# Attention with a condition token: turning blocks of x later, one head's row scores ahead in all phases, the maxima split between two halves of an exchange

## The chip, the cores and the metric

The kernel runs on one core of one Trainium2 chip. The metric is the device time of one execution in microseconds (us); lower is better. Three runs of the kernel before took 650.82 to 651.73 us, the median is 651.13 us. The profile comes from one execution of its own, which took 652.28 us; its span, from the first to the last instruction, is 650.4 us. In the profile PE is TensorE's matmuls, PEld its weight loads, DVE VectorE, ACT ScalarE, POOL GpSimd, SP SyncE.

## What is computed

x is (8, 512, 512) in float32: 8 batches, 512 positions, 512 channels in 16 heads of 32. A condition token per batch adds its own projections to queries and keys, and the attention's output is added to x.

```python
Q = _split_heads(x @ Wq.T + bq)
K = _split_heads(x @ Wk.T + bk)
V = _split_heads(x @ Wv.T + bv)
tQ = _split_heads(tokens @ Wq.T + bq)
tK = _split_heads(tokens @ Wk.T + bk)
cQ = Q + tQ
cK = K + tK
scores = jnp.einsum('bhqd,bhkd->bhqk', cQ, cK) / jnp.sqrt(jnp.float32(HEAD_DIM))
attn = jax.nn.softmax(scores, axis=-1)
out = jnp.einsum('bhqk,bhkd->bhqd', attn, V)
return out.transpose(0, 2, 1, 3).reshape(B, S, D_MODEL)
...
x = x + _L0_cond_ref(x, cond_1024[:, None, :], L0_cond_Wq, L0_cond_bq, L0_cond_Wk, L0_cond_bk, L0_cond_Wv, L0_cond_bv)
```

## The kernel before

**Groups and phases.** Four heads make a group; 8 batches of 4 groups give 32 groups t = 0 to 31. The groups run as a pipeline written out by hand: every engine executes its instructions in the order in which the program emits them, and waits on semaphores for what it needs. A start covers the first projections and group 0, then the function thirds (from L1152) runs once for each of t = 1 to 28, and a tail written out for the last three groups ends the kernel. One call of thirds is called a phase here. Even and odd are by t; r is t modulo 4.

**Row scores, maxima, denominators.** For the softmax each row's maximum is needed first. row_scores (L640) computes the scores of 128 queries by 512 keys of one head into one bank of PSUM; four heads take four banks. VectorE takes the negated maxima (one_max, L592, one bank; row_max_of, L649, two neighbouring banks at once). denominators (L700) has ScalarE compute exp(score + negated maximum) with the sum along the row. For the first two of four query blocks these exponentials are kept in SBUF (the tile store) and used; for the other two only the sums are.

**Kept exponentials and the exchange.** The kept ones lie with queries on the partitions, and the product with V needs keys there. turn_kept (L659) turns blocks of 32 by 32 on VectorE; then swap_kept (L681) exchanges the blocks between partition groups by DMA in three rounds (move 0: part to a place aside; move 1: counterpart to part; move 2: aside to counterpart), each of six DMAs of 128 KB. Move 1 is issued by SyncE, move 2 by GpSimd, move 0 by both: with `later = 6 if t % 4 == 1 else 2`, the first 2 (or all 6) by SyncE and the rest by GpSimd. Each DMA waits for the round before it to land.

**The other half.** For the last two query blocks the scores are computed again, transposed: the maxima have been split into three bfloat16 parts by four small GpSimd instructions (split_max, L714 to L717), turned by one DMA that SyncE issues (turn_max, L726), and less_max (L771) adds them into PSUM by a matmul; scores_of_rest (L784) adds the scores, and ScalarE takes the exponential (rest_leaves, L798). In odd phases joined does this for i = 1 and puts row scores of one head (number 1) between less_max and the first scores_of_rest, and the other three heads' row scores before the last of them. In even phases exponentials_of_rest comes first and all four heads' row scores behind it.

**One phase** has three parts. i = 0: row scores and maxima of group t + 1's query blocks 1 and 2, then the product with V of group t - 1 (weighted: L839 sums, L874 spreads the denominators, L911 turns the result, L912 and L913 scale it and add x, L916 stores it), then one of the items of projection. i = 1 and i = 2: the second half's exponentials of group t, the row scores of (t + 1, block 3) and (t + 2, block 0), and one more item each. The projections (L461) of the next batch are spread over four phases in twelve items (MADE), each six to eight small products of a Strassen-like scheme; q, k and v items end in VectorE, ScalarE or GpSimd instructions (first_by_others, L529 to L540; other_products, L554 and L486; other_shared, L1230 to L1236). The last L486 of an even phase's i = 1 makes the keys that the row scores of i = 2 read.

**Banks.** The eight banks of PSUM go round by lists: row_of says which bank has which role in a part, released(...) says in which order the roles pass on to the next, and begin(...) moves a pair of neighbouring banks to the end of each four.

**x.** Blocks of x come by four DMAs each (load_block, L173, SyncE), two tiles in turn; turn_x (L371) turns one block into xT on VectorE. turn_more calls it once per phase, in i = 0, behind weighted (place (0, 2)); load_blocks right behind it loads the block after next into the tile that has just been read, which waits for the turn. combine_x has GpSimd make sums of parts of xT in every fourth phase. The tile pool xtp has two tiles for xT, taken in turn by batches. So SyncE's queue has in each phase: its share of moves 0 and 1, four stores of the result, four loads of x, the DMA that turns the maxima, four loads of the residual (L191), in this order.

Of the kernel before, what the change touches and what calls it, by code (L numbers as in the profile page):

```python
# [9 lines left out]
F32 = mybir.dt.float32  # L10
# [7 lines left out]
def kernel(  # L18
# [38 lines left out]
    nc = tc.nc  # L57
# [18 lines left out]
    xp = ctx.enter_context(tc.tile_pool(name="xp", bufs=2))  # L76
    xtp = ctx.enter_context(tc.tile_pool(name="xtp", bufs=2))
    qkp = ctx.enter_context(tc.tile_pool(name="qkp", bufs=3))
# [268 lines left out]

    xT = {}

    def transpose_x(n, pt, leaves=nc.vector.tensor_copy):  # L350

        b, sc = divmod(n, NS)
        if b >= B:
            return
        if sc == 0:
            xT[b] = xtp.tile([P, NC, S], F32, tag="xT", name=f"xT_{b}")
        for cc in range(NC):
            nc.tensor.transpose(
                pt[:, cc * P : (cc + 1) * P], xs[n][:, cc * P : (cc + 1) * P], ident
            )  # L360
        leaves(xT[b][:, :, sc * P : (sc + 1) * P], pt.rearrange("p (c s) -> p c s", c=NC))
        if n > 1:
            load_block(n + 2)

    def turn_x(n):
        b, cc = divmod(n, NC)
        if b >= B:
            return
        if cc == 0:
            xT[b] = xtp.tile([P, NC, S], F32, tag="xT", name=f"xT_{b}")  # L370
        nc.vector.transpose(xT[b][:, cc, :], xs[n].rearrange("p f i -> p (f i)"))  # L371
        to_load.append(n + 2)

    to_load = []

    def load_blocks():
        while to_load:
            load_block(to_load.pop(0))
# [701 lines left out]
    bias_residual(1)  # L1080
    turn_x(NC + 3)
    load_blocks()
    advance()
# [3 lines left out]
    other_products("v", 0, 0, nothing, nothing, (0, 2))  # L1087
    turn_kept(1, 0)
    advance()
# [4 lines left out]
    first_products("v", 0, 1, lambda: denominators(1, 3), nothing, 1)  # L1094
    turn_kept(1, 1)
    turn_kept(1, 2)
# [43 lines left out]
    TURNED_LAST = {(0, 2): 2, (1, 2): 2}  # L1140
    turned = {}

    def turn_more(t, i, after):

        for _ in range((TURNED if t + 1 < KEPT[-1] else TURNED_LAST).get((i, after), 0)):
            if t + 1 in KEPT:
                n = turned[t + 1] = turned.get(t + 1, -1) + 1
                turn_kept(t + 1, n)
        if (i, after) == (0, 2):
            turn_x((t - 1) % G + ((t - 1) // G + 2) * NC)  # L1150

    def thirds(t, made):  # L1152
# [12 lines left out]
        turn_more(t, 0, 2)  # L1165
        load_blocks()
        one_item(of, *next(made), (2, 3), ignore, nothing)
        released(0, 1, 4, 5, 6, 7, 2, 3)
        for i in (1, 2):
            begin(HG)  # L1170
            rows = (t + 1, 3) if i == 1 else (t + 2, 0)
            if i == 1 and r % 2 == 1:
                joined(t, i - 1, rows)
# [7 lines left out]
            if i == 1:  # L1181
                first = range(6 if t + 1 < KEPT[-1] else 3)
                swap_kept(t, 2, first)
# [17 lines left out]
            if i == 1:  # L1201
                aparts[t] = masked(t)
            load_blocks()
            if (t + 1, i) == (KEPT[-1], 1):
# [232 lines left out]
    two = [slice(0, HS), slice(HS, S)]  # L1437
    nc.vector.tensor_tensor(part_x[:, two[0]], pd[:, two[0]], xr[t][:, two[0]], ALU.mult)
    nc.scalar.copy(den, pd)
    store_30(nc.scalar, (2, 3))  # L1440
    oT = late_part(4)
# [5 lines left out]
    for i in range(2):  # L1447
        nc.vector.tensor_tensor(oT[:, two[i]], pv[:, two[i]], part_x[:, two[i]], ALU.add)  # L1448
        if i == 0:
            nc.vector.tensor_tensor(part_x[:, two[1]], pd[:, two[1]], xr[t][:, two[1]], ALU.mult)  # L1450
        for qc in (i * 2, i * 2 + 1):
# [48 lines left out]
```

## Time and profile before

| what | value |
|---|---|
| median of 3 runs | 651.13 us (650.82 to 651.73) |
| the profiled execution | 652.28 us, span 650.4 us |
| TensorE matmuls busy | 643.4 us (99%) |
| VectorE busy | 598.4 us (92%) |
| ScalarE busy | 534.3 us (82%) |
| GpSimd busy | 409.6 us (63%) |
| DMA engines' time taken by SyncE's queue | 53.4% |
| DMA engines' time taken by GpSimd's queue | 19.7% |
| mean granted TensorE clock | 1.000 |
| start of phase t = 8, seen by ScalarE's L631 | 202.80 us |
| start of phase t = 22 | 471.28 us |

Matmul ends are modelled, so TensorE's busy share says little; the weight loads (PEld) show when TensorE could begin. In a timeline each row has a start, a duration, engine, line, operation, what is written and read, the shape, how many alike are merged, and in brackets how long the engine was idle before it and what ended that. The releaser is inferred; where the one named had long been done, it was another.

### The profile page before, as it was taken

Reading aid. Unit: us, or ns where it says so; the run is one execution under the profiler, and the core shown is the slowest. Engines: PE = TensorE matmul, PEld = TensorE weight load, DVE = VectorE, ACT = ScalarE, POOL = GpSimd, SP = SyncE. Lnnn points to the kernel's source line nnn. Section 1 sums busy time; section 2 is a strip of 40 time slices with the busy share of each in tenths; the row PEclk is TensorE's granted clock in tenths of the full one; section 3 lists DMA queues with packets and bytes.
Section 4 is the critical chain, followed back from the end, with each engine's and each line's share of the span. In section 5 each row is a group of like instructions: output and inputs, shape, how many; then the busy total and the mean of one; then the engine's idle time right before and its main releaser. Section 6 shows DMA issues by size and latency. Waiting matters only on the chain. (4 is left out here: it accounts for less than half of the span.)

```text
span 650.4 us, 24900 instructions
## 1 busy us (share of the span) xinstructions
PE 643.4 (99%) x9856; PEld 352.8 (54%) x9856; DVE 598.4 (92%) x846; ACT 534.3 (82%) x1364; POOL 409.6 (63%) x651
## 2 busy tenths in 40 slices
PE   9999999999999999999999999999999999999997
PEld 8444555556555555555555555555655555555541
DVE  3799999999999999999999999999998999999887
ACT  2479888889888889888888988898987888888564
POOL 3642555787656875767676676667666677675650
PEclk9999999999999999999999999999999999999999
DMA  7624588878878888877887777896888887887921
GB/s 188 108 47 65 116 183 175 164 172 181 180 163 179 168 169 180 186 163 159 180 173 164 180 155 172 176 195 136 178 159 163 191 177 152 168 180 155 205 35 33
DMA packets 248456, 102.01 MB, mean 157 GB/s; under 512 B 229962, under 2 KB 230474, under 8 KB 248340
## 3 DMA queue, kind: packets, MB, share of 16 engines
q1 hardware_dynamic: 234196, 65.54, 53.4%
q0 software_dynamic: 12384, 33.83, 19.7%
q8 instruction: 78, 1.28, 0.9%
q10 hardware_dynamic: 1760, 1.05, 0.5%
q14 instruction: 38, 0.31, 0.2%
HBM read 19.75 MB, written 8.39 MB: 43 GB/s over the span
## 5 line engine op out<-in xcount | busy, mean ns | idle before, releaser
L592 DVE TENSOR_REDUCE nmax<-psum 128x1 f32<-128x512 f32 x279 | 177.0, 677 | 11.0 <-PE psum L640 6.2
L700 ACT ACTIVATE psum<-psum,nmax 128x512 f32<-128x512 f32 x248 | 164.7, 672 | 3.8 <-DVE nmax L592 3.0
L700 ACT ACTIVATE store<-psum,nmax 128x512 f32<-128x512 f32 x204 | 139.5, 700 | 25.9 <-DVE nmax L592 25.3
L681 POOL DMA_DIRECT2D store<-store x258 | 128.5, 502 | 46.9 <-DMA store<-store 26.7
L640 PE MATMUL psum<-kT,qT 32*128 32x512 f32 x1024 | 150.8, 612 | 0.0
L798 ACT ACTIVATE store<-psum 128x512 f32<-128x512 f32 x232 | 119.8, 603 | 34.3 <-PE psum L784 34.3
L659 DVE STREAM_TRANSPOSE store<-store 128x1024 f32<-128x1024 f32 x116 | 138.9, 1217 | 0.0
L649 DVE TENSOR_REDUCE nmax<-psum 128x2 f32<-128x1024 f32 x98 | 118.9, 1213 | 0.0
L839 PE MATMUL psum<-store,v 128*32 128x256 f32 x1856 | 106.8, 381 | 0.0
L839 PEld LDWEIGHTS psum<-store,v 128*32 128x32 f32 x1856 | 57.0, 110 | 57.1 <-ACT wT_q L631 21.2
L912 POOL TENSOR_TENSOR res<-res,recs 128x512 f32<-128x512 f32 x30 | 31.3, 1045 | 84.5 <-DVE res L911 84.4
L640 PEld LDWEIGHTS psum<-kT,qT 32*128 32x128 f32 x1024 | 56.8, 183 | 36.4 <-issue 18.0
L784 PE MATMUL psum<-qT,kT 32*128 32x256 f32 x928 | 71.9, 373 | 0.0
L784 PEld LDWEIGHTS psum<-qT,kT 32*128 32x128 f32 x928 | 53.1, 184 | 4.8 <-issue 0.3
L700 ACT ACTIVATION_READ_ACCUMULATOR psum<-psum,nmax 128x1 f32 x248 | 53.4, 215 | 0.0
L461 PE MATMUL psum<-wc_v,xc 128*32 128x256 f32 x768 | 47.7, 379 | 0.0
L204 POOL TENSOR_TENSOR xr<-xr,bvs 128x512 f32<-128x512 f32 x30 | 38.5, 1282 | 10.4 <-DMA xr<-in_x_dram 10.4
L461 PE MATMUL psum<-xc,wc_q 128*32 128x256 f32 x720 | 44.7, 379 | 0.0
L461 PE MATMUL psum<-xc,wc_k 128*32 128x256 f32 x720 | 44.5, 379 | 0.0
L700 ACT ACTIVATION_READ_ACCUMULATOR store<-psum,nmax 128x1 f32 x204 | 44.3, 217 | 0.0
L913 POOL TENSOR_TENSOR res<-res,xr 128x512 f32<-128x512 f32 x30 | 38.3, 1276 | 2.4
L461 PE MATMUL psum<-xT,wT_k 128*32 128x256 f32 x480 | 34.5, 382 | 0.0
(192 smaller groups left out, 971.9 us busy)
## 6 DMA issues: line engine op xcount, KB each, us to landing
store<-store SPq DMA_DIRECT2D x264, 128.0 KB, 2.9
store<-store POOLq DMA_DIRECT2D x258, 128.0 KB, 3.9
out_dram<-res SPq DMA_DIRECT2D x122, 64.0 KB, 3.7
xr<-in_x_dram SPq DMA_DIRECT2D x120, 64.0 KB, 2.7
x<-in_x_dram SPq DMA_DIRECT2D x112, 64.0 KB, 3.9
w_q<-in_L_cond_Wq_dram SPq DMA_DIRECT2D x4, 256.0 KB, 3.8
w_v<-in_L_cond_Wv_dram SPq DMA_DIRECT2D x16, 64.0 KB, 2.5
w_k<-in_L_cond_Wk_dram SPq DMA_DIRECT2D x16, 48.0 KB, 2.8
```

Source lines behind the costliest of these rows:

```text
L204: nc.gpsimd.tensor_tensor(xr[t], xr[t], bias, ALU.add)
L461: nc.tensor.matmul(pt[r], still[:, r], moving, start=(kc == kcs[0]), stop=(kc == kcs[-1]))
L592: nc.vector.tensor_reduce(nmax[t][:, qc, j : j + 1, 0], pt, AX.X, ALU.max, negate=True)
L640: nc.tensor.matmul(pt, qkT["q", t][r, qc * P : (qc + 1) * P], qkT["k", t][r, :], start=True, stop=True,)
L649: nc.vector.tensor_reduce(nmax[t][:, qc, pr * 2 : pr * 2 + 2, 0], pt, AX.X, ALU.max, negate=True)
L659: nc.vector.transpose(e, e)
L681: (nc.gpsimd if here else nc.sync).dma_start(to, of)
L700: nc.scalar.activation(to, of, AF.Exp, bias=nmax[t][:, qc, j, :], accum_out=sums[t][:, qc, j, :],)
L784: nc.tensor.matmul(banks(j)[:, i * HS : (i + 1) * HS], qkT["k", t][r, kc * P : (kc + 1) * P], qkT["q", t][r, KQ * P :], start=False, stop= ...
L798: nc.scalar.activation(e[:, j], banks(j), AF.Exp)
L839: nc.tensor.matmul(pt[j * HD : (j + 1) * HD, half * HS : (half + 1) * HS], vs[b % 2][:, kc, (g * HG + j) * HD : (g * HG + j + 1) * HD], e, ...
L913: nc.gpsimd.tensor_tensor(y, y, xr.pop(t), ALU.add)
```

## The change

- turn_more turns a block of x at place (2, 1) (behind the maxima of i = 2) in even phases, and at (0, 2) as before in odd ones; t = 2 does both, so that from there on each block is turned one phase earlier in the count of blocks. The order of blocks is kept by a counter.
- load_blocks loads at most one block, at its old place in i = 0; the second call at the end of each part is gone. What it loads then has its tile free from the phase before or from this one.
- xT is one tile for both batches, so that slices are waited for singly.
- joined is used for i = 1 in all phases. The banks of i = 0 are passed on with two roles exchanged (7, 6 for 6, 7).
- Of the six GpSimd DMAs of move 2, three stand ahead of split_max and turn_max and three behind; before, all six stood ahead (but in the last phase, where it was three already).
- In the start, the turn of the fourth block of batch 1 and its load move behind the next products, and two turns of kept exponentials move one place forward.
- In the tail, ScalarE's copy of the denominators goes ahead of VectorE's multiplication, which is one instruction over 512 columns and no longer two over 256.

```diff
-    xtp = ctx.enter_context(tc.tile_pool(name="xtp", bufs=2))
...
+    xT_both = const.tile([P, 2, NC, S], F32, tag="xT", name="xT")
...
-            xT[b] = xtp.tile([P, NC, S], F32, tag="xT", name=f"xT_{b}")
+            xT[b] = xT_both[:, b % 2]
...
-    def load_blocks():
-        while to_load:
+    def load_blocks(most=B * NC):
+        for _ in range(min(most, len(to_load))):
             load_block(to_load.pop(0))
...
-    turn_x(NC + 3)
-    load_blocks()
+    turn_kept(1, 0)
     advance()
     exponentials(0, 1)
     row_max(1, 2)
     denominators(1, 2)
     other_products("v", 0, 0, nothing, nothing, (0, 2))
-    turn_kept(1, 0)
+    turn_x(NC + 3)
+    load_blocks()
+    turn_kept(1, 1)
...
     first_products("v", 0, 1, lambda: denominators(1, 3), nothing, 1)
-    turn_kept(1, 1)
     turn_kept(1, 2)
...
+    next_x = [2 * NC]
...
-        if (i, after) == (0, 2):
-            turn_x((t - 1) % G + ((t - 1) // G + 2) * NC)
+        even = t % 2 == 0
+        if (i, after) == ((2, 1) if even else (0, 2)) or (t, i, after) == (2, 0, 2):
+            turn_x(next_x[0])
+            next_x[0] += 1
...
         turn_more(t, 0, 2)
-        load_blocks()
+        load_blocks(1)
         one_item(of, *next(made), (2, 3), ignore, nothing)
-        released(0, 1, 4, 5, 6, 7, 2, 3)
+        released(0, 1, 4, 5, 7, 6, 2, 3)
...
-            if i == 1 and r % 2 == 1:
+            if i == 1:
                 joined(t, i - 1, rows)
...
             if i == 1:
-                first = range(6 if t + 1 < KEPT[-1] else 3)
+                first = range(3)
                 swap_kept(t, 2, first)
                 split_max(t + 1)
                 turn_max(t + 1)
...
-            load_blocks()
...
-    nc.vector.tensor_tensor(part_x[:, two[0]], pd[:, two[0]], xr[t][:, two[0]], ALU.mult)
     nc.scalar.copy(den, pd)
+    nc.vector.tensor_tensor(part_x, pd, xr[t], ALU.mult)
...
-        if i == 0:
-            nc.vector.tensor_tensor(part_x[:, two[1]], pd[:, two[1]], xr[t][:, two[1]], ALU.mult)
```

More of the change, by code (lines that the diff above doesn't have):

```diff
@@ L369, in turn_x @@
         if cc == 0:
-            xT[b] = xtp.tile([P, NC, S], F32, tag="xT", name=f"xT_{b}")
+            xT[b] = xT_both[:, b % 2]
         nc.vector.transpose(xT[b][:, cc, :], xs[n].rearrange("p f i -> p (f i)"))
```

## The prediction

> **What bounds the kernel now.** I read the page first, then the weight loads of TensorE in order of time, since TensorE looks full.
>
> ```profile
> span 650.4 us, 24900 instructions
> PE 643.4 (99%) x9856; PEld 352.8 (54%) x9856; DVE 598.4 (92%) x846; ACT 534.3 (82%) x1364; POOL 409.6 (63%) x651
> ```
>
> A busy share of 99% leaves no hole to fill on that row, but matmul ends are modelled; what TensorE really does is seen in the gaps between weight loads. 28 of the 32 groups of four heads go through one loop (the function thirds), about 19.2 us a phase. This is an even phase (t = 10), its second and third parts (i = 1 and i = 2); columns: start, duration, what, and in brackets idle time and releaser.
>
> ```profile
> 248.27 0.10 PEld L771 LDWEIGHTS <-onesb 3*128 3x128 bf16 x4 [0.41 <-issue]
> 249.15 0.41 PEld L640 LDWEIGHTS psum<-kT,qT 32*128 32x128 f32 x8
> 250.32 0.59 PEld L461 LDWEIGHTS psum<-xc,wT_k 128*32 128x32 f32 x16 [0.76 <-ACT store L798]
> 253.48 0.10 PEld L771 LDWEIGHTS <-onesb 3*128 3x128 bf16 x4 [0.41 <-issue]
> 254.60 0.34 PEld L640 LDWEIGHTS psum<-kT,qT 32*128 32x128 f32 x8 [0.26 <-ACT psum L700]
> 255.71 0.59 PEld L461 LDWEIGHTS psum<-wT_v,xc 128*32 128x32 f32 x16 [0.76 <-ACT store L798]
> ```
>
> And the same of the odd phase behind it (t = 11), which already has one head's row scores ahead:
>
> ```profile
> 267.92 0.10 PEld L771 LDWEIGHTS <-onesb 3*128 3x128 bf16 x4 [0.41 <-DMA store<-store]
> 269.97 0.59 PEld L461 LDWEIGHTS psum<-xc,wT_q 128*32 128x32 f32 x16 [0.34 <-ACT store L798]
> 273.13 0.10 PEld L771 LDWEIGHTS <-onesb 3*128 3x128 bf16 x4 [0.41 <-issue]
> 274.01 0.41 PEld L640 LDWEIGHTS psum<-kT,qT 32*128 32x128 f32 x8
> ```
>
> The reader is to see three things. First, 0.41 and 0.76 return at every change between score matmuls and column matmuls, with whatever releaser: they belong to the change itself. Second, part i = 1 takes 253.48 - 248.27 = 5.21 us in the even phase and 273.13 - 267.92 = 5.21 us in the odd one. From its first load to the first product load it is 2.05 us in both (250.32 - 248.27; 269.97 - 267.92): the interleaved burst is longer by what its gap is shorter. Third, the only wait that one phase has and the other has not is 254.60: the row scores of i = 2 begin 1.12 us after that part's start, in the odd phase 0.88 us (274.01 - 273.13). So **TensorE's own order bounds the loop**, and the even phases lose up to 0.24 us at one place.
>
> What ends that wait? The brackets name ScalarE, but the row scores of head group t + 2 read keys that VectorE's last L486 makes in this same phase:
>
> ```profile
> 247.41 2.32 DVE L659 STREAM_TRANSPOSE store<-store 128x1024 f32<-128x1024 f32 x2
> 249.66 0.67 DVE L371 STREAM_TRANSPOSE xT<-x 128x512 f32<-128x512 f32 x1
> 250.42 1.29 DVE L592 TENSOR_REDUCE nmax<-psum 128x1 f32<-128x512 f32 x2
> 253.09 1.40 DVE L486 SCALAR_TENSOR_TENSOR kT<-psum,tok,kT 128x512 f32<-128x512 f32 x2
> 256.97 1.22 DVE L649 TENSOR_REDUCE nmax<-psum 128x2 f32<-128x1024 f32 x1
> 258.74 0.42 DVE L1232 TENSOR_TENSOR v<-psum,v 128x256 f32<-128x256 f32 x1 [0.56 <-ACT aside L1230]
> 259.44 0.69 DVE L1234 TENSOR_TENSOR v<-psum,v 128x512 f32<-128x512 f32 x1 [0.27 <-PE psum L461]
> ```
>
> L486 ends at 253.09 + 1.40 = 254.49, 0.11 us ahead of 254.60: it is the releaser. VectorE runs without a hole from 247.41 to there.
>
> **The change part by part.** *The turn of x (0.67 us) leaves the even phases' first part.* Does that alone pull L486 forward? Phase t = 26 has no block of x left to turn, so the trace shows it:
>
> ```profile
> 558.32 1.29 DVE L592 TENSOR_REDUCE nmax<-psum 128x1 f32<-128x512 f32 x2 [0.69 <-PE psum L640]
> 560.99 1.40 DVE L486 SCALAR_TENSOR_TENSOR kT<-psum,tok,kT 128x512 f32<-128x512 f32 x2
> ```
>
> ```profile
> 561.38 0.10 PEld L771 LDWEIGHTS <-onesb 3*128 3x128 bf16 x4 [0.41 <-issue]
> 562.44 0.31 PEld L640 LDWEIGHTS psum<-kT,qT 32*128 32x128 f32 x8 [0.20 <-DVE kT L486]
> ```
>
> No: L486 ends at 562.39, 1.01 us after the part's start, as in t = 10 (254.49 - 253.48 = 1.01). The time of the turn becomes 0.69 us of waiting for row scores. Alone it is worth 0; it is the early head that lets VectorE begin.
>
> *One head's row scores ahead in even phases* (14 more uses of joined). TensorE issues the same 16 + 8 score loads; the burst costs 0 by the two equal 2.05 us. VectorE can take that head's maximum when its two L659 end (249.73), 0.69 us before 250.42, and then waits for the products instead: as in the odd phase,
>
> ```profile
> 273.33 0.75 DVE L486 SCALAR_TENSOR_TENSOR qT<-psum,tok,qT 128x512 f32<-128x512 f32 x1 [0.17 <-PE psum L461]
> ```
>
> L486 ends 273.33 + 0.75 - 273.13 = 0.95 us after the part's start in place of 1.01. That is 0.06 us, and no more, since TensorE's last product now sets it. Of the 0.24 us the rest stays, because the keys are needed. Even phases t = 2 to 22 have this wait, 11 of them, the first and the last:
>
> ```profile
> 100.85 0.34 PEld L640 LDWEIGHTS psum<-kT,qT 32*128 32x128 f32 x8 [0.32 <-ACT psum L700]
> ...
> 484.70 0.34 PEld L640 LDWEIGHTS psum<-kT,qT 32*128 32x128 f32 x8 [0.27 <-ACT psum L700]
> ```
>
> t = 2 keeps a turn in its first part, so I count ten: 10 x 0.06 = **0.6 us gained**. In t = 24, 26 and 28 the load already stands at 562.44 - 561.38 = 1.06 us: following the bank lists by hand, the first row-score bank there is one that VectorE itself frees, so the load waits for one engine. With the swapped release (7, 6) that bank is in every even phase one that ScalarE frees, two engines to wait for, and 254.60 stands 0.11 us behind L486's end where 562.44 stands 0.05. So these three lose up to 0.05 us each: **0.1 us lost**. Bounds of this part: below, the whole 0.24 us in 14 phases, 3.4 us; above, a product start that slips as far as in odd phase t = 9,
>
> ```profile
> 229.53 0.10 PEld L771 LDWEIGHTS <-onesb 3*128 3x128 bf16 x4 [0.41 <-DMA store<-store]
> 231.62 0.62 PEld L461 LDWEIGHTS psum<-xc,wT_q 128*32 128x32 f32 x16 [0.38 <-POOL qT L538]
> ```
>
> 2.09 us, and with its slower first loads about 0.07 us in each of 14, 1.0 us. I take -0.6 + 0.1 = -0.5 us, nearest to the odd rows of t = 11.
>
> The Trainium skill has a rule against my equal 2.05 us. TensorEngine Tiling (Array Packing), section Key Properties, says that changing the tiling mode drains TensorE. By it alone the 0.34 in place of 0.76 would be 0.42 us a phase of gain; the rows agree that a drain is there, but show the burst longer by the same amount.
>
> *The turn of x at (2, 1) of even phases* (0.67 us). It stands behind 256.97 + 1.22 = 258.19, ends at 258.86, and L1232 begins 0.12 us later than 258.74, ends by 259.29; L1234 starts at 259.44 in any case. Cover: the pauses of 0.56 and 0.27 us; cost 0, and if ScalarE's copy came earlier, at most 0.12 us a phase. It may write there because xT is now one tile whose slices are waited for singly: the first slice's last reader is the product of i = 0. Queued behind it: L1232, L1234, then the next phase's row scores.
>
> *Loads of x.* SyncE issues the same four DMAs a phase at the same place, behind the output's four and ahead of the maxima's transposing DMA. They no longer wait for a turn of the same phase, and each lands about one phase before its turn instead of two. Cover: that phase; without it a late block holds VectorE at L371, as at the start (0.79 us, below). 0.
>
> *Maxima split behind three of six exchange DMAs.* On GpSimd the four split instructions come earlier, and three DMAs later by their length, 1.2 us (from the end of the six DMAs, 488.61, to the split's end, 489.84, in the rows below). The transposing DMA on SyncE still stands behind the loads of x:
>
> ```profile
> 485.49 3.12 POOL L681 DMA_DIRECT2D store<-store  x6 [3.92 <-DMA store<-store]
> ...
> 489.57 0.27 POOL L717 TENSOR_TENSOR split<-rest,split 128x16 bf16<-128x16 f32 x1
> ```
>
> ```profile
> 488.42 4.36 SPq L173 DMA_DIRECT2D x<-in_x_dram  x4
> 492.88 1.25 SPq L726 DMA_TRANSPOSE maxT<-split  x1
> ```
>
> The split is ready at 489.84, SyncE reaches the DMA at 492.88. Value at first hand 0; the queues are a rival below.
>
> *Start and end.* At the start this turn moves behind the next maxima and products, and an exchange turn of 1.2 us (half of 2.32 above) moves ahead of them:
>
> ```profile
> 52.52 0.71 DVE L371 STREAM_TRANSPOSE xT<-x 128x512 f32<-128x512 f32 x1 [0.79 <-DMA x<-in_x_dram]
> ```
>
> VectorE then waits for no block there, 0.71 + 0.79 us out and 1.2 us in. I count 0, within 0.3 us less (the difference) and 0.7 us more (a turn of 0.71 us later laid bare). At the end ScalarE's copy of 0.58 us goes ahead and one 512-wide multiplication replaces two of the length of L1448:
>
> ```profile
> 644.75 0.58 ACT L1439 COPY store<-psum 128x512 f32<-128x512 f32 x1 [2.36 <-DVE store L1438]
> 645.83 0.42 DVE L1448 TENSOR_TENSOR store<-psum,store 128x256 f32<-128x256 f32 x1
> ```
>
> The copy waited for VectorE's read of the same bank; reversed, VectorE waits 0.58 us, then needs about 0.69 us (as L1234): the second L1448 ends at 646.2 to 646.4 against 646.25 now. I take 0.
>
> **The sum.** -0.6 + 0.1 + 0 = -0.5 us. The profiled execution took 652.28 us (span 650.4 and 1.9 around it), the median 651.13; the same edits would take that execution to 651.8; forecast for the median 651.13 - 0.5 = 650.6 us. About 0.2%, 1.3 us, is what a measurement here can tell from no change, so the bounds are 649.8 and 652.4.
>
> **The rivals.** *The queues' lag goes.* SyncE falls behind in the loop:
>
> ```profile
> 217.84 1.62 SPq L726 DMA_TRANSPOSE maxT<-split  x1
> ```
>
> ```profile
> 202.80 0.58 ACT L631 COPY wT_q<-psum 128x512 f32<-128x512 f32 x1 [0.32 <-PE psum L640]
> 471.28 0.58 ACT L631 COPY wT_q<-psum 128x512 f32<-128x512 f32 x1 [0.32 <-PE psum L640]
> ```
>
> In 14 phases its DMA moves 492.88 - 217.84 = 275.0 us, the phases 268.5: 0.47 us of lag a phase. At the end of that TensorE is late twice:
>
> ```profile
> 493.04 1.48 PEld L839 LDWEIGHTS psum<-store,v 128*32 128x32 f32 x32 [0.25 <-issue]
> 499.22 0.10 PEld L771 LDWEIGHTS <-onesb 3*128 3x128 bf16 x4 [1.61 <-DMA maxT<-split]
> ```
>
> The second is 1.61 - 0.41 = 1.2 us, the first up to 0.25. GpSimd waited 3.92 us for landings ahead of the split; if three suffice, it reaches the next exchange up to 1.25 us sooner, SyncE waits less, and both go: -0.5 - 1.4 = -1.9, **649.2 us**. For it: the waits. Against: SyncE's number of DMAs is unchanged, and the profiled execution is 1.15 us above the median, so the median may not hold these waits at all.
>
> *The later half of the exchange is late* (the other side). Where all six have landed at once, as at 485.49, the last three are issued 1.25 us later, and the weighted sums at 493.04 already wait for the last of them. From a lag like that of t = 20 to 22 on, TensorE pays about 1 us each, three times, 3.0 - 0.5 = 2.5: **653.6 us**. For it: the 0.25 at 493.04. Against: in most phases there are microseconds of room.
>
> *The early head costs in even phases* as in t = 9: +1.0 in place of -0.5, **652.1 us**, no change by the bound.
>
> *The drain saved in full:* the early head shortens the gap of 0.76 us to 0.34 and the burst stays as short as in even phases now: 14 x 0.42 = 5.9 us, **645.2 us**. For it: the two gaps; against it: the two equal 2.05 us. This is the time by the Trainium skill's rule named above.
>
> *The change does nothing:* VectorE has slack anyway, 651.1 us.
>
> **How the numbers follow.** Forecast 0.45, of which 0.06 beyond the bound; lag gone 0.24; exchange late 0.13; early head costs 0.09; nothing 0.06; drain 0.03. Faster: 0.24 + 0.06 + 0.03 = 0.33; slower 0.13 + 0.02 = 0.15; the same 0.52. The range takes in the lag's case and the costly head, and leaves out the drain, the late exchange's far end and a little of each tail: 648.7 to 652.8.
>
> **What would show it.** L640 of i = 2 in even phases at 1.06 us after L771; L371 between L649 and L1232 there; part i = 1 still 5.21 us; the gap before L771 near 498 us gone or not; L839's second half with or without idle time ahead of it. I am wrong if i = 1 changes its length, or if TensorE waits for DMAs in more than two phases.

## The result and the profile after

The changed kernel is **slower by 0.4%**: median 653.68 us (651.1 to 657.98, 14 runs) against 650.96 us (650.19 to 652.62, 14 runs), ratio 1.0041, 95% interval 1.0024 to 1.0058. Its times spread over 7 us where the kernel before spreads over 2.4 us. The forecast was 650.6 us (648.7 to 652.8). The profiled execution of the changed kernel took 652.65 us, less than the median; what the longer executions lose is in no trace. Medians below are over all executions of a kernel and ratios over its fast ones alone, so the two can part (e2, e8, e12).

The first lines of its page tell nothing of this; TensorE's busy share is again 99%:

```profile
span 650.6 us, 24881 instructions
PE 642.1 (99%) x9856; PEld 358.0 (55%) x9856; DVE 601.2 (92%) x845; ACT 533.9 (82%) x1364; POOL 413.4 (64%) x651
```

**The loop does what was forecast.** These are TensorE's weight loads of the changed kernel's phase t = 10, the phase that the prediction shows of before (start, duration, what, and the idle time ahead with its releaser):

```profile
246.43 0.10 PEld L771 LDWEIGHTS <-onesb 3*128 3x128 bf16 x4 [0.41 <-DMA store<-store]
248.48 0.59 PEld L461 LDWEIGHTS psum<-xc,wT_k 128*32 128x32 f32 x16 [0.34 <-ACT store L798]
251.63 0.10 PEld L771 LDWEIGHTS <-onesb 3*128 3x128 bf16 x4 [0.41 <-issue]
253.80 0.59 PEld L461 LDWEIGHTS psum<-wT_v,xc 128*32 128x32 f32 x16 [0.76 <-ACT store L798]
```

```profile
252.70 0.34 PEld L640 LDWEIGHTS psum<-kT,qT 32*128 32x128 f32 x8 [0.20 <-ACT psum L700]
```

Part i = 1 takes 251.63 - 246.43 = 5.20 us, from its first load to the first product 2.05 us, as before: the interleaved burst is longer by what its gap is shorter. In i = 2 the row scores begin 252.70 - 251.63 = 1.07 us behind the part's start (1.12 before, 1.06 forecast). VectorE turns the block of x behind the maxima, and the next addition follows at once:

```profile
255.06 1.22 DVE L649 TENSOR_REDUCE nmax<-psum 128x2 f32<-128x1024 f32 x1
256.19 0.70 DVE L371 STREAM_TRANSPOSE xT<-x 128x512 f32<-128x512 f32 x1
256.90 0.42 DVE L1234 TENSOR_TENSOR v<-psum,v 128x256 f32<-128x256 f32 x1
257.53 0.69 DVE L1236 TENSOR_TENSOR v<-psum,v 128x512 f32<-128x512 f32 x1 [0.20 <-PE psum L461]
```

**The start gains.** Phase t = 2 begins (ScalarE's L631) 1.28 us earlier; the first row is the kernel before, the second the changed one:

```profile
87.37 0.58 ACT L631 COPY wT_q<-psum 128x512 f32<-128x512 f32 x1 [0.33 <-PE psum L640]
```

```profile
86.09 0.59 ACT L631 COPY wT_q<-psum 128x512 f32<-128x512 f32 x1 [0.33 <-PE psum L640]
```

**The time is lost in the weighted sums.** Their 64 loads come as one burst of 3.18 us where all blocks of the kept exponentials have landed in time. In the changed kernel's profile three phases (t = 16, 17 and 23) have a hole in the middle, ahead of the half that reads them:

```profile
355.01 1.45 PEld L839 LDWEIGHTS psum<-store,v 128*32 128x32 f32 x32 [0.76 <-ACT wT_q L631]
358.59 1.48 PEld L839 LDWEIGHTS psum<-store,v 128*32 128x32 f32 x32 [2.12 <-issue]
...
376.05 1.45 PEld L839 LDWEIGHTS psum<-store,v 128*32 128x32 f32 x32 [0.76 <-ACT wT_q L631]
378.88 1.22 PEld L839 LDWEIGHTS psum<-store,v 128*32 128x32 f32 x25 [1.38 <-issue]
...
492.09 1.45 PEld L839 LDWEIGHTS psum<-store,v 128*32 128x32 f32 x32 [0.76 <-ACT wT_q L631]
494.50 1.48 PEld L839 LDWEIGHTS psum<-store,v 128*32 128x32 f32 x32 [0.96 <-issue]
```

From one first load of L839 to the next these phases take 1.87, 1.15 and 0.65 us more than their like, 3.67 us together. "issue" is what the view prints where no semaphore event explains the wait; the landings do. The six DMAs of move 2 for the first of the three, on GpSimd's queue and from the view of their line:

```profile
348.19 1.52 POOL L681 DMA_DIRECT2D store<-store  x3 [2.14 <-DMA out_dram<-res]
...
351.15 1.49 POOL L681 DMA_DIRECT2D store<-store  x3 [0.21 <-issue]
```

```profile
DMA to landing us min/median/max: 2.4/2.9/6.0
```

The slowest took 6.0 us; issued as the last one at 352.1 it is there at 358.1, and the second half begins at 358.59. The kernel before has its 64 loads of that phase without a hole.

In this largest hole the landing is slow, and not the issue late: the last DMA is issued 2.9 us ahead of the first load at 355.01, and 2.8 us ahead in e13 below, which has no hole there and whose slowest took 3.7 us. In the two smaller holes both have grown. The last DMA is issued 2.6 and 3.5 us ahead of the first load (e13: 5.65 in both), and the slowest of the last three took 5.0 and 5.6 us (e13: 3.0 and 3.4).

**SyncE's queue has another order.** The prediction, and the description ahead of it, took it that SyncE issues its DMAs as the text has them. It does not: the loads of x, which no longer wait for a turn of the same phase, stand elsewhere than in the text. As far as the runs show, a DMA's place follows from what it has to wait for (e13 below gives the loads a late reader to wait for, and they are back in the old place). First the kernel before, then the changed one, at the same phase (t = 15):

```profile
336.87 2.17 SPq L191 DMA_DIRECT2D xr<-in_x_dram  x4
339.22 8.64 SPq L681 DMA_DIRECT2D store<-store  x8
347.95 3.45 SPq L916 DMA_DIRECT2D out_dram<-res  x4
351.50 3.18 SPq L173 DMA_DIRECT2D x<-in_x_dram  x4
354.79 1.44 SPq L726 DMA_TRANSPOSE maxT<-split  x1
```

```profile
336.62 1.61 SPq L172 DMA_DIRECT2D x<-in_x_dram  x3
338.40 7.84 SPq L681 DMA_DIRECT2D store<-store  x8
346.33 3.58 SPq L916 DMA_DIRECT2D out_dram<-res  x4
349.96 0.75 SPq L172 DMA_DIRECT2D x<-in_x_dram  x1
350.75 0.52 SPq L190 DMA_DIRECT2D xr<-in_x_dram  x1
351.38 1.32 SPq L726 DMA_TRANSPOSE maxT<-split  x1
```

Three of the four loads (1.61 us) have moved up, directly ahead of the moves of the exchange; from phase to phase it is two to four. Where SyncE has no idle time left, moves 0 and 1 are issued that much later, move 2 waits for them to land, and of move 2 the second half now stands behind the split too.

### The profile page after: what moved, and what is told of

It reads as the page before. It is cut to its first block, busy times and chain, and to the rows that moved or that the text cites. A ratio compares the mean times of both kernels' runs of the same rounds, so it can differ in the third digit from the quotient of the medians.

```text
span 650.6 us, 24881 instructions
## 1 busy us (share of the span) xinstructions
PE 642.1 (99%) x9856; PEld 358.0 (55%) x9856; DVE 601.2 (92%) x845; ACT 533.9 (82%) x1364; POOL 413.4 (64%) x651
## 3 DMA queue, kind: packets, MB, share of 16 engines
q8 instruction: 78, 1.28, 0.9%
## 5 line engine op out<-in xcount | busy, mean ns | idle before, releaser
L640 PE MATMUL psum<-kT,qT 32*128 32x512 f32 x1024 | 161.8, 612 | 0.0
L839 PE MATMUL psum<-store,v 128*32 128x256 f32 x1856 | 107.4, 381 | 3.1 <-DMA xr<-in_x_dram 2.2
L839 PEld LDWEIGHTS psum<-store,v 128*32 128x32 f32 x1856 | 57.3, 110 | 60.6 <-ACT wT_q L631 21.2
L784 PE MATMUL psum<-qT,kT 32*128 32x256 f32 x928 | 83.8, 373 | 0.0
L640 PEld LDWEIGHTS psum<-kT,qT 32*128 32x128 f32 x1024 | 61.3, 183 | 35.4 <-issue 17.8
L784 PEld LDWEIGHTS psum<-qT,kT 32*128 32x128 f32 x928 | 60.8, 184 | 5.7 <-issue 0.3
L700 ACT ACTIVATION_READ_ACCUMULATOR psum<-psum,nmax 128x1 f32 x248 | 55.1, 222 | 0.0
```

The source lines that it names most:

```text
L640: nc.tensor.matmul(pt, qkT["q", t][r, qc * P : (qc + 1) * P], qkT["k", t][r, :], start=True, stop=True,)
L700: nc.scalar.activation(to, of, AF.Exp, bias=nmax[t][:, qc, j, :], accum_out=sums[t][:, qc, j, :],)
L784: nc.tensor.matmul(banks(j)[:, i * HS : (i + 1) * HS], qkT["k", t][r, kc * P : (kc + 1) * P], qkT["q", t][r, KQ * P :], start=False, stop= ...
L839: nc.tensor.matmul(pt[j * HD : (j + 1) * HD, half * HS : (half + 1) * HS], vs[b % 2][:, kc, (g * HG + j) * HD : (g * HG + j + 1) * HD], e, ...
```

## The experiments

Five theories. **A**: the split amid the exchange alone makes the second half of move 2 late. **B**: the new place of the loads of x alone does. **C**: only both together use up the room. **D**, formed on the first results: SyncE's queue has almost no free time in a phase of 19.15 us; what lengthens it makes a lag at the exchange's moves. **E**, its rival: the traffic of the DMA engines makes landings late, wherever a DMA is issued. Of C, **C1** says that the loads' place in SyncE's queue counts, **C2** the turns' new place on VectorE or more traffic at a time.

A measure for D, worked out from the traces in each of 24 phases: the start of SyncE's first move of the exchange minus the first load of L839 (0.1 us when SyncE has been waiting for VectorE's turn, more when it comes late). In the changed kernel's phase t = 16, where all four loads stand ahead of the moves, it is 5.02 us, from 355.01 above and

```profile
356.27 3.59 SPq L172 DMA_DIRECT2D x<-in_x_dram  x4
360.03 1.71 SPq L681 DMA_DIRECT2D store<-store  x2
```

### One suspect at a time

**e1_split_behind_six.** The changed kernel with

```diff
-                first = range(3)
+                first = range(6 if t + 1 < KEPT[-1] else 3)
```

> The changed kernel, but the maxima are split behind all six exchange DMAs of move 2 again. Theory A (the three later DMAs of move 2 are issued 1.2 us later on GpSimd and land too late for the second half of the weighted sums): the waits of 2.1 us at L839 go, the spread of the runs narrows, 649.5 to 650.3 us, a ratio of 0.998 to the kernel before. Theory B (the loads of x, which no longer wait for a turn, were put elsewhere in SyncE's queue, behind the transposing DMA and the residual's loads, and meet the next exchange): as the changed kernel, 653 to 654 us. Theory C (both are needed, the one makes landings slower and the other takes the room away): as A here.

Measured: 650.02 us, ratio to the kernel before 0.9987 (0.9977 to 0.9997). B falls.

**e2_split_alone.** The kernel before with `first = range(3)`, the same edit the other way.

> The kernel before with one edit: three of six DMAs of move 2 ahead of the split in all phases. Theory A: L839's second half waits as in the changed kernel, 653 to 654.5 us. Theory B: as the kernel before, 651 us. Theory C: as the kernel before, within 0.5 us.

Measured: 651.2 us, ratio 1.0005 (0.9997 to 1.0014); one of the twelve executions took 2299.93 us, for a reason that nothing here shows, and is not in the ratio. A falls.

**e3_x_alone.** The kernel before with

```diff
+    xT_both = const.tile([P, 2, NC, S], F32, tag="xT", name="xT")
...
-        if (i, after) == (0, 2):
-            turn_x((t - 1) % G + ((t - 1) // G + 2) * NC)
+        even = t % 2 == 0
+        if (i, after) == ((2, 1) if even else (0, 2)) or (t, i, after) == (2, 0, 2):
+            turn_x(next_x[0])
+            next_x[0] += 1
...
-        load_blocks()
+        load_blocks(1)
...
-            load_blocks()
```

> The kernel before with only the turns of x and their loads as in the changed kernel (xT one tile, turn at (2, 1) in even phases, one load per phase). SyncE's queue then holds most loads of x behind the transposing DMA and the residual's loads, three of four ahead of the exchange's moves. Theory A: as the kernel before, 650.5 to 651.3 us, the move 2 landings unchanged. Theory B: landings of move 2 late, 653 to 654 us. Theory C: 650.5 to 651.5 us, landings later by some tenths but in time.

Measured: 651.08 us, ratio 1.0003 (0.9994 to 1.0012).

**e6_after_x_as_before.** The changed kernel with `if (i, after) == (0, 2)` for the turns and `load_blocks()` behind them.

> The changed kernel, but x is turned at (0, 2) in all phases and loaded right behind, so that SyncE's queue has its old order; the split stands amid the exchange. Theory A: still slow, 652.5 to 654 us with waits at L839. Theory B: 649.5 to 650.5 us. Theory C: 649.5 to 650.5 us.

Measured: 649.89 us, ratio 0.9985 (0.9976 to 0.9994). Each suspect alone costs nothing that can be told, taking away either turns the changed kernel's loss into a gain: C. e7 completes the square.

**e7_neither.** The changed kernel with both edits, e1's and e6's.

> The changed kernel with both suspects undone: split behind all six DMAs, x turned at (0, 2) and loaded right behind in all phases. Joined scores, start and tail stay as changed. By theory C the two harm only together, and what is left gains by itself what it gains beside either: 649.6 to 650.3 us. If the split amid the exchange has a worth of its own (SyncE's lag of 0.47 us a phase gone), this one is slower than the kernel with only the split, by up to 1 us: 650.5 to 651 us.

Measured: 649.93 us, ratio 0.9987 (0.9979 to 0.9996): the split amid the exchange is worth nothing in time by itself. Ratios to the kernel before, with the rest of the change in all four:

| | loads of x as before | as changed |
|---|---|---|
| split behind six | 0.9987 | 0.9987 |
| split amid | 0.9985 | **1.0041** |

The measure for D in the traces, as the number of 24 phases in which SyncE is over 2 us late, and the latest:

| | loads of x as before | as changed |
|---|---|---|
| split behind six | before: 7, 6.0 us; e7: 7, 5.4 us | e3: 16, 6.7 us; e1: 16, 5.9 us |
| split amid | e2: 0, 1.5 us; e6: 0, 0.9 us | changed: 5, 5.0 us |

e4 and e5 below also have the split behind six and the loads as before, and show 8 phases, 4.3 us, and 14 phases, 5.9 us: one trace a kernel is not enough to tell the two columns of the upper row apart. In the lower row the split lets SyncE go on sooner, and the loads hold it up.

The lag alone does not say what a phase loses. e1 and e3 have more of it than the changed kernel, their last DMAs of move 2 are issued no earlier (4.3 and 4.5 us ahead of the next first load in the median, the changed kernel's 5.1), and their five holes are 0.1 to 0.4 us each, 1.5 us in all. In no phase of theirs does one of the last three take over 5.5 us to land; in the three holes above it is 6.0, 5.0 and 5.6 us, on DMAs issued 2.6 to 3.5 us ahead. That the loss comes only with both changes is shown by the times. Why slow landings then meet late issues is not shown.

### The parts that were to gain

**e4_joined_alone.** The kernel before with

```diff
-            if i == 1 and r % 2 == 1:
+            if i == 1:
...
-        released(0, 1, 4, 5, 6, 7, 2, 3)
+        released(0, 1, 4, 5, 7, 6, 2, 3)
```

> The kernel before with only the early head in even phases and the banks passed on as 7, 6. By the prediction's step 0.5 us less, 650.3 to 650.6 us, L640 of i = 2 at 1.06 us after L771; by the drain's rule 5.9 us less, 645 us; by the rival of late products 1 us more, 652 us.

Measured: 650.48 us, ratio 1.0001 (0.9992 to 1.001): not to be told from no change. In its trace L640 of i = 2 begins 253.98 - 252.92 = 1.06 us behind L771,

```profile
252.92 0.10 PEld L771 LDWEIGHTS <-onesb 3*128 3x128 bf16 x4 [0.41 <-issue]
252.93 0.85 PEld L784 LDWEIGHTS psum<-qT,kT 32*128 32x128 f32 x16
253.98 0.34 PEld L640 LDWEIGHTS psum<-kT,qT 32*128 32x128 f32 x8 [0.20 <-ACT psum L700]
```

and from the first load of L839 to the 27th the loop takes 498.15 us, in e2 (whose loop has the same single wait of 0.36 us) 498.72 us: 0.57 us gained where 0.5 was forecast.

**e5_start_alone.** The kernel before with the turns and the load of the start in the changed order.

> The kernel before with only the start in its new order. The prediction said 0 (0.3 less to 0.7 more); the changed kernel's trace, in which phase 1 begins 1.28 us earlier, says 1.0 to 1.3 us less: 649.6 to 650 us.

Measured: 650.43 us, ratio 0.9996 (0.9987 to 1.0004): not to be told from no change. The first load of L839 stands at 88.21, 87.69, 87.90 and 87.88 us in the four profiles with the old start (mean 87.92), at 86.94 to 88.14 in the eleven with the new one and no new tile (mean 87.49): 0.4 us, or 0.6 without the two latest (e9 and e16). Most of the 1.28 us that the two profiles show is chance. From the 27th first load to the end it is 62.23 to 62.26 us with the old tail, 62.15 to 62.21 with the new in the seven kernels whose edits leave the end alone.

### Is it the place of the loads in SyncE's queue?

**e8_loads_tied.** The changed kernel with a new tile of 4 bytes a partition and

```diff
+        if to_load and to_load[0] - 2 in xs:
+            nc.gpsimd.tensor_copy(tie, xs[to_load[0] - 2][:, 0, 0:1])
         load_blocks(1)
```

> The changed kernel with one thing added: in each phase, ahead of the load of x, GpSimd copies one column of the block of x that the load overwrites (behind its two products for the result), so that the load has something to wait for and stands in SyncE's queue behind the stores of the result and ahead of the transposing DMA again. Turns, joined scores and split stay as changed. Theory C1 (the loads' place in the queue: three of four stand directly ahead of the exchange's moves and delay them by about 1.7 us): the waits at L839 go, 649.5 to 650.5 us. Theory C2 (the new place of the turns on VectorE, or more DMA traffic at a time, delays the exchange): 652.5 to 654 us still.

Measured: 658.86 us (651.38 to 662.22), ratio 1.0094 (1.0065 to 1.0123), with SyncE's queue in the order of before and over 2 us late in 20 of 24 phases. Against C1, and against C2 too, which had no reason for more than 654.

**e12_tie_old_turns.** e6 with the same tile and copy.

> The changed kernel with x turned at (0, 2) in all phases (as in the kernel with x as before, 649.9 us) and with GpSimd's one-column copy ahead of the loads as in the tied one (658.9 us). SyncE's queue has the same order in all three. If GpSimd's copy or the wait for it made the tied kernel slow: 655 to 660 us. If the new place of the turns did, or loads that land one phase ahead of their turn and no longer right behind it: 649.6 to 650.4 us.

Measured: 659.64 us, ratio 1.015 (1.011 to 1.019). So the tie did it, or what came with it: the new tile takes 32 bytes of each partition, and the tiles behind it, most of those that DMAs read and write, begin 32 bytes later.

**e14_tile_shifted.** e6 with the tile alone, filled once and never used:

```diff
+    tie = const.tile([P, 1], F32, tag="tie", name="tie")
+    nc.gpsimd.memset(tie, 0.0)
     xT_both = const.tile([P, 2, NC, S], F32, tag="xT", name="xT")
```

> The kernel with x as before and the split amid the exchange (649.9 us) with one new tile of 4 bytes a partition that is filled once at the start and never used: the tiles behind it begin 32 bytes later, nothing else changes. If the addresses made the tied kernels slow (transfers between tiles that begin at 32 beyond a multiple of 64 take longer): SyncE late at the moves by 3 to 6 us from the first phases on, 655 to 660 us. If not: 649.6 to 650.3 us.

Measured: 655.25 us, ratio 1.0074 (1.0049 to 1.0099), 5.4 us above e6: the shift by itself. In the built programs (no trace shows addresses) the tiles x, xr, res and store begin at multiples of 128 bytes of a partition, and 32 beyond with the new tile. The same packets take longer. Those of 4096 bytes in SyncE's queue, the exchange's, take 283 ns in the mean in this trace and 288 to 289 ns in the three other kernels with such a shift (e8, e10, e12); in the fifteen without, 260 to 279 ns. The queue's share of the DMA engines' time is a poorer sign: in e6, then in e14 (packets, MB, share), it is

```profile
q1 hardware_dynamic: 234196, 65.54, 55.0%
```

```profile
q1 hardware_dynamic: 234196, 65.54, 57.6%
```

but 55.5% in e8 and 54.3% in e12. SyncE is over 2 us late in 8 phases (e6: none). The Trainium skill has a reason that fits (DMA: Bandwidth & Descriptors, section How a descriptor splits into AXI transactions): each transaction of a transfer has to start at a multiple of 256 bytes, so that a piece which crosses such an address, without starting at one, can take one transaction more. The traces agree with more time for the same packets; no run here shows the cutting itself.

**e13_tied_no_new_tile.** e8 once more, its copy into a tile that the loop doesn't use otherwise:

```diff
+            nc.gpsimd.tensor_copy(condT[:, 0, 0:1], xs[to_load[0] - 2][:, 0, 0:1])
```

> The tied kernel once more, but GpSimd's one-column copy goes into a tile that is there already and is not used any more in the loop (condT), in place of a new tile. The new tile moved every tile behind it by 32 bytes: the tiles that DMAs read and write began at multiples of 64 bytes in the kernel before and in the changed one, and in the tied one at 32 beyond. Theory C1 or D with the place in the queue as the cause of the changed kernel's loss: 649.5 to 650.5 us. If GpSimd's read, or the wait for it, made the tied kernel slow: 655 to 660 us again.

Measured: **649.24 us** (648.9 to 651.71, 12 runs), ratio 0.9981 (0.9973 to 0.999). Turns, bytes, split and heads are those of the changed kernel; only the place of the loads is the old one:

```profile
336.86 7.90 SPq L681 DMA_DIRECT2D store<-store  x8
344.85 2.21 SPq L916 DMA_DIRECT2D out_dram<-res  x4
347.15 3.62 SPq L172 DMA_DIRECT2D x<-in_x_dram  x4
351.53 1.22 SPq L726 DMA_TRANSPOSE maxT<-split  x1
```

```profile
355.56 3.18 PEld L839 LDWEIGHTS psum<-store,v 128*32 128x32 f32 x64 [0.76 <-ACT wT_q L631]
```

The last three DMAs of move 2 for that phase, and the landing of all six, which the changed kernel's hole was compared with:

```profile
351.71 1.50 POOL L681 DMA_DIRECT2D store<-store  x3 [0.21 <-issue]
```

```profile
DMA to landing us min/median/max: 2.4/3.1/3.7
```

SyncE is never over 1.4 us late, the 64 loads come in one burst, and the spread is gone (11 of 12 runs within 1.1 us). So of C1 and C2 it is C1: with the same DMAs, the order of SyncE's queue decides.

### Room in the queue, or traffic?

**e11_quarter_by_scalar.** The changed kernel, one of the four loads on ScalarE's queue:

```diff
+                queue = nc.scalar if h == 3 and n >= 2 * NC + 4 else nc.sync
...
             if i == 1:
+                load_blocks(1)
                 joined(t, i - 1, rows)
```

> The changed kernel, but ScalarE issues one of the four loads of x per phase, ahead of the exponentials of i = 1, where it waits for TensorE; SyncE's queue is shorter by 0.6 us a phase and two of three loads stand ahead of the moves in place of three of four. Theory D: SyncE's lag at the moves falls by about 0.6 us and does not build up, 649.5 to 651.5 us, unless ScalarE lays its issue bare, 0.1 to 0.5 us in 24 phases. Theory E: 652.5 to 654 us.

Measured: 649.48 us, ratio 0.9978 (0.9968 to 0.9988); never over 2 us late. As D says, with the same traffic. But not two of the three loads left on SyncE stand ahead of the moves, as expected, but all three:

```profile
354.07 2.81 SPq L173 DMA_DIRECT2D x<-in_x_dram  x3
```

That is as many as in the changed kernel in the mean of its phases. The place alone does not make the loss, then; it takes the length of the queue with it. The Trainium skill (DMA: Bandwidth & Descriptors, section Issuing engines are not separate DMA queues) calls the time that a second issuing engine saves usually small beside the DMA itself; here some 0.6 us a phase less of it on SyncE is worth 4 us of 654.

**e10_one_load_more.** e6 with one DMA of 16 KB more per phase ahead of the moves.

> The kernel with x as before and the split amid the exchange (649.9 us, SyncE at the moves on time in all phases), and one more DMA per phase: 16 KB of x into a tile that is not used for the result, in SyncE's queue between the residual's loads and the moves. Theory D: 0.5 to 0.6 us more of issuing in each phase, more than the idle time of 0 to 0.8 us there in about half of them; the lag appears and stays, 652 to 658 us. Theory E: 16 KB beside 3.3 MB a phase is nothing, 649.7 to 650.3 us.

Measured: 663.88 us, ratio 1.0179 (1.0153 to 1.0204). It too had new tiles, which moved the others to 32 beyond a multiple of 64, so it can't be read for D.

**e15_one_load_more_no_tile.** The same DMA into the idle condT, and a one-column copy on GpSimd that it waits for:

```diff
+                nc.sync.dma_start(condT[:, 0, :], x[0, 0:P, 0:BL])
             else:
+                nc.gpsimd.tensor_copy(condT[:, 1, 0:1], condT[:, 0, 0:1])
```

> The kernel with one DMA of 16 KB more per phase ahead of the moves, but into condT, without a new tile. Theory D (SyncE's queue has room for less than one DMA more in a phase): lag at the moves that builds up, later landings, 650.5 to 655 us; the part of the 663.9 us that goes is the addresses'. Theory E (only bytes count): 649.6 to 650.3 us.

Measured: 651.03 us, ratio 1.0007 (0.9999 to 1.0016), 1.1 us above e6; over 2 us late in 5 phases, at most 3.3 us. The lag is as D says, half a microsecond of issuing per phase being more than the room, but it costs little: in the profiles the loop is only 0.3 us longer than e6's (498.51 and 498.19), and 0.6 us are lost behind the 27th first load.

**e9_x_by_gpsimd.** The changed kernel, the loads of x on GpSimd's queue ahead of `weighted`.

> The changed kernel, but in the loop GpSimd issues the four loads of x, in its pause ahead of the products for the result. Bytes and turns are the same; SyncE's queue is shorter by four DMAs a phase (some 2.5 us of issuing). Theory D (SyncE's queue has almost no room in a phase of 19.15 us, so that what stands ahead of the moves makes a lag that the late half of move 2 cannot bear): SyncE reaches the moves on time in all phases, no waits at L839, 649 to 650 us. Theory E (the DMA engines' traffic, not the issuing, makes landings late): 652.5 to 654 us or more. If GpSimd pays much more than 0.6 us for one of these DMAs of 128-byte pieces, its own queue becomes late and neither can be read.

Measured: 674.64 us, ratio 1.0372 (1.0346 to 1.0397). The new place was ahead of the turn of odd phases, and the block turned there had been loaded in the same phase; from the view of waits:

```profile
DVE xT L371 <- DMA x<-in_x_dram: 22.0, 11, 2.8
```

**e17_x_by_gpsimd_ahead.** e9 with one block more loaded in t = 2, so that each load is one phase ahead of its turn.

> As the run in which GpSimd issues the loads of x (674.6 us), but each load one phase ahead of its turn; there the odd phases turned a block whose load had been issued in the same phase, and VectorE waited 22.0 us for landings in 11 phases. Here SyncE loads one block more behind the second turn of t = 2. Theory D (room in SyncE's queue decides): SyncE at the moves on time in all phases, no waits at L839, 649 to 650 us. Theory E (traffic decides): L839 waits as in the changed kernel, 652.5 to 654 us. If GpSimd's 2.6 us of issuing in its pause of 3.2 us makes its products for the result late: 1 to 3 us more than D.

Measured: 655.53 us, ratio 1.0073 (1.0052 to 1.0094), and yet the loop is as D says: SyncE at most 0.3 us late, one wait of 0.3 us at L839, the loop 498.13 us (e13 498.07, changed kernel 501.55). The 6.7 us are lost behind the 27th first load, where 68.88 us stand in place of 62.17; of that 4.5 us behind the last work. The first and the last line of the chain's view, of e17 and then of e13:

```profile
core 0 of [0], span 654.3 us
...
646.38 0.33 DVEq L1497
```

```profile
core 0 of [0], span 647.5 us
...
644.07 0.33 DVEq L1497
```

From the last work to the span's end it is 654.3 - 646.71 = 7.6 us, in e13 647.5 - 644.40 = 3.1 us.

**e16_tied_and_quarter.** e13 with e11's quarter.

> The changed kernel with the loads of x tied as in the run without a new tile (649.2 us), and with one of the four loads issued by ScalarE as in the run with the quarter (649.5 us). If SyncE's lag is all that the two remove, the second adds nothing to the first: 649.0 to 649.4 us. If some of the other phases still lose to late landings, 648 to 649 us.

Measured: 661.84 us, ratio 1.0168 (1.0154 to 1.0182). SyncE is on time, but ScalarE now waits in its own queue for GpSimd's copy, ahead of the exponentials that TensorE needs:

```profile
312.91 0.19 POOL L1171 COPY condT<-x 128x1 f32<-128x1 f32 x1
```

```profile
313.13 0.32 ACTq L173 DMA_DIRECT2D x<-in_x_dram  x1
313.50 2.06 ACT L799 ACTIVATE store<-psum 128x512 f32<-128x512 f32 x4 [1.07 <-PE psum L785]
```

The phases are longer by about 0.4 us and 0.8 us in turn, as long as there are blocks to load. Two remedies that cure the same thing don't add, and the wait of the one lay bare in the queue of the other.

## Why the prediction was wrong

- **The step that failed** is "Loads of x. SyncE issues the same four DMAs a phase at the same place", put at 0. The place was read off the text; freed of the turn, three of the four moved up, ahead of the moves (1.61 us in the rows above). e13 puts back this alone, by one small GpSimd copy a phase, and is some 4 us faster than the changed kernel (ratios 0.9981 and 1.0041).
- "Maxima split behind three of six exchange DMAs: value at first hand 0" holds alone (e2 1.0005; e6 against e7), not beside the loads (1.0041 against 0.9987). That the 1.25 us by which the last three come later are room that the loads' lag needs fits two of the three holes; in the largest the issue is as early as in e13.
- The rival **"The later half of the exchange is late"** came true in its place: TensorE waits ahead of L839's second half in three phases, by 1.87, 1.15 and 0.65 us where about 1 us each was forecast, and "TensorE waits for DMAs in more than two phases" too. Its mechanism is half right: the split alone costs nothing (e2), and the largest hole comes of a slow landing. That 653.6 us was forecast and 653.68 measured is luck; the changed kernel's runs spread over 7 us. The rival had a chance of only 0.13, since its room was read from a queue whose order was assumed.
- The rival "The queues' lag goes" is right in its mechanism: with the split amid, SyncE is over 2 us late in none of 24 phases instead of 7 (e2, e6). Its 1.4 us are not: e2's median is no better, which fits the prediction's doubt that the median of before holds those waits. The lag of 0.47 us a phase was a mean, too: by the measure above, SyncE is at most 0.5 us late from t = 8 to 13 of the kernel before and 1.0 to 6.0 us from t = 14 to 22.
- Early heads: -0.5 forecast, -0.57 in the loop of e4. The burst of equal 2.05 us held; the drain's 5.9 us (the Trainium skill's rule that the prediction names) and "early head costs" fall: the gap is 0.34 us in place of 0.76, and part i = 1 as long as before. In time of the whole kernel e4 shows no change clear of noise (1.0001). The turn of x at (2, 1) costs 0: even phases take 19.15 us with and without it.
- Start: 0 forecast, -0.4 to -0.6 by the traces; mis-sized, outside its bound of -0.3, though e5's time does not show it clear of noise. Tail: 0 forecast, -0.07.

One gain the prediction had not: phase t = 5 takes 19.17 us in e13 and the changed kernel, 19.52 in the kernel before and e6, where x is turned as before. With the loads tied, the sum would be -0.5 for the heads, -0.1 for the tail, -0.4 to -0.6 for the start and -0.35 for that phase, -1.35 to -1.55 us; e13 measured -1.27 against its own runs of the kernel before.

Still open: why that one DMA took 6.0 us to land and not 3.7 as the slowest at the same place in e13. It is not issued later, and the DMA engines move no more bytes then (167 GB/s from 352.0 to 358.5 us, in e13 187 GB/s from 352.5 to 359.0); no run separates what else lands beside it. Why e12 is 4 us slower than e14, although the same copy costs nothing in e13. And why in phase t = 15 the last DMAs of move 2 are issued some 2 us late in the profiles of e2, e6 and e13, where SyncE is otherwise on time, but not in that of e17.

## What to carry to other kernels

Where a queue's order follows from what its DMAs wait for, taking a wait away from a DMA moves it: look at what it now stands ahead of, not at its line in the text. Two changes that each spend room of the same transfer have to be priced together, by the least room of any phase, and here a wide spread of run times (7 us in place of 2.4) came with the loss. When an experiment needs a new tile, put it where it moves no other tile, or test the tile alone.

## What the runs showed of the hardware

- Tiles that begin 32 bytes beyond a multiple of 128 in place of at one: 5.4 us (0.9985 to 1.0074; e6, e14), with 283 to 289 ns in place of 260 to 279 for a packet of 4096 bytes in SyncE's queue.
- SyncE's issuing is nearly full here: one DMA of 16 KB more per phase makes it up to 3.3 us late (e15; 0.9 us in e6) and costs 1.1 us.
- Loads of x by GpSimd took 5.2 us from issue to landing in the median (e9; 4.9 us in e17), by SyncE 3.7 us (e6; 2.9 us in the changed kernel). With 84 of them on GpSimd's queue (e17) the program's end, behind the last work, took 7.6 us in place of 3.1 (e13); with 88 (e9) it took 8.0.

```profile
x<-in_x_dram POOLq DMA_DIRECT2D x88, 64.0 KB, 5.2
```

```profile
x<-in_x_dram SPq DMA_DIRECT2D x112, 64.0 KB, 3.7
```
